# Four graph layers on one core: new adjacency landing times in the planner, and the last layer's weights folded later

## The chip, the cores and the metric

The kernel runs on one core of a Trainium2 chip. The metric is the time of one execution on the device in microseconds (us), lower is better. The engines are named as in the profile: PE is TensorE (PEld its weight loads), DVE is VectorE, ACT is ScalarE, POOL is GpSimd, and SP is the queue that issues most of the DMA transfers.

## The reference

32 graphs of 512 nodes with 128 features each share one 512x512 adjacency matrix `adj` of zeros and ones. Four layers follow one another, each behind a layernorm with ReLU and with a residual:

```python
# every layer: h = maximum(layernorm(x), 0);  x = x + layer(h)
# layer 0, attention: x_h = elu(h @ Wi + bi)
e = sigmoid(a_tgt[:, :, None] + a_src[:, None, :] + be) * (adj + 0.005 * (adj == 0))
agg = einsum('bij,bjh->bih', e, x_h);  self_part = x_h * sum(e, -1)
out = concat([elu(concat([agg, self_part]) @ Wn + bn), x_h]) @ Wm + bm
# layer 1, gated recurrence, 5 steps with in_matrix = out_matrix = adj
m = adj @ h;  av = concat([m, m]);  u3 = h @ u3_w.T
z = sigmoid(av @ w3_w.T + u3);  r = sigmoid(av @ w4_w.T + u3)
h = (1 - z) * h + z * tanh(av @ w5_w.T + (r * h) @ u5_w.T)
# layer 2: adj @ (h @ weight) + bias
# layer 3: weight_1 is 128 x 128 x 7; both adjacencies are adj, so
#   y = h @ w[:,:,0] + sum over k = 1..3 of adj^k h @ (w[:,:,k] + w[:,:,k+3])
```

In layer 3 the same powers of `adj` come twice, so that pairs of the seven weight slices can be added beforehand. These sums are the folded weights V[1] to V[3]; V[0] is the first slice alone.

## The kernel before

**Tiles.** The graphs are taken in eight groups of four. A tile of 512 columns holds one graph, either by token or by feature. The adjacency is loaded once in four chunks `A_nat` (L412), two on the SP queue and two on ACT's, and turned by 16 transposes (`adjacency_turned`, L601). DVE counts the entries that are neither zero nor one (`n_odd`, L592), PE adds the counts up (`count`, L621), and every engine reads the result and branches on it (L1184): with a binary adjacency the first arm runs. There `adj` goes through PE in the fp32r form, the other operand as a high and a low part (`parts`, L981), and the square of the adjacency is made at L974. Products with the small weights are full fp32 (`product`, L513).

**The order of the work.** Nothing is scheduled at run time. Every step is entered in a list with `op(engine, us, due, emit, reads, writes, ...)`: the engine, a cost in us, a due time and the tiles. `Plan.order` (L155) plays this list through with the costs and with landing times (`RESULT`, L76, or `result=` of a step), and each engine always takes the ready step with the earliest `turn`, which is its due time plus a `shift`. A step can't begin if its turn lies more than 110 us behind the oldest open one. What comes out is one fixed list of instructions for each engine; on the chip an engine works through its own list and waits at semaphores. A step whose input is late on the chip therefore holds up everything behind it on its engine.

Three things bend the order by hand. `A_LANDS` (L319) says when the four adjacency chunks are taken to land. `HEAD_NUDGES` (L25) is a list of seeds; for each, `nudge` (L255) adds random shifts of some us to steps that are due between 0 and 130, and `TAIL_NUDGES` does so behind 1430. And while the plan has no step for PE in its first 50 us (`FILL`), it puts in `plan.idle` (L375), a product of two tiles of ones into a spare bank, which nothing reads.

**Steps near the change.** Buffers are handed out by the plan: 38 `f` tiles of 128x512, eight PSUM banks `b`, five `x` groups, and so on. A layernorm is moments on DVE (L553 to L556), a power of -1/2 on POOL (L558), a small DVE operation (L562) and a scaling on ACT (L567). Between layouts by token and by feature a tile goes through DRAM: blocks are transposed on DVE (L462) and carried by two transfers (L464, then L475, L494 or L499). From the fifth graph on, a row of attention scores is spread over all partitions in the same way (`as_row`, L658). Sums over sources run as adding transfers on the POOL queue (`totals`, L672, and L802). The V tiles are made at L952: for each half of the outputs SP loads 448 columns of the raw weights into an `f` tile, and POOL makes four pieces from it, a copy (L960) and three additions (L962). They are read by `token_products` (L1093) in layer 3.

Of the kernel before, what the change touches and what calls it, by code (L numbers as in the profile page):

```python
# [21 lines left out]


HEAD, TAIL = 250.0, 1430.0
HEAD_NUDGES = (7100008, 7100429, 7300015, 7100544, 7100583, 7300139, 7300091, 7300684, 7300016, 7300033, 7300035,  # L25
    7300041, 7300077, 7300137, 7300140, 7300167, 7300172, 7300174, 7300178, 7300506, 7300199,
    7300249, 7300263, 7300279, 7300298, 7300305, 7300507, 14000074, 14000497, 7300344, 7300346,
    7300367, 7300389, 7300391, 7300393, 7300406, 7300423, 14000795, 7300482, 7300509, 7300510,
    7300530, 7300532, 7300539, 7300544, 14000157, 7300549, 7300551, 7300553, 7300562, 7300570,
    14000024, 14000577, 7300614, 7300629, 7300644, 14000027, 14000360, 7300654, 7300663, 7300681,  # L30
    14000347, 7300696, 14000026, 14000010, 14000014, 14000195, 14000023, 14000035, 14000039,
    14000042, 14000045, 14000046, 14000048, 14000088, 14000208, 14000563, 14000122, 14000125,
    14000164, 14000166, 14000167, 14000181, 14000182, 14000252, 14000186, 14000187, 14000189,
    14000198, 14000204, 14000210, 14000212, 14000213, 14000739, 14000219, 14000227, 14000231,
    14000243, 14000275, 14000289, 14000299, 14000304, 14000306, 14000385, 14000319, 14000324,
    14000325, 14000326, 14000333, 14000338, 14000345, 14000346, 14000355, 14000358, 14000364,
    14000665, 14000398, 14000472, 14000417, 14000426, 14000427, 14000432, 14000438, 14000440,
    14000451, 14000458, 14000463, 14000469, 14000485, 14000486, 14000515, 14000520, 14000521,
    14000647, 14000528, 14000531, 14000540, 14000596, 14000560, 14000561, 14000815, 14000569,
    14000570, 14000580, 14000589, 14000591, 14000597, 14000602, 14000605, 14000606, 14000609,  # L40
    14000629, 14000638, 14000654, 14000661, 14000689, 14000678, 14000681, 14000685, 14000686,
    14000697, 14000698, 14000700, 14000703, 14000708, 14000715, 14000716, 14000721, 14000723,
    14000725, 14000726, 14000732, 14000734, 14000744, 14000751, 14000753, 14000755, 14000788,
    14000796, 14000801, 14000804, 14000807, 14000808, 14000811, 14000816, 14000817, 14000818,
    14000822, 14000827, 14000829, 14000831, 14000836, 14000839, 14000842, 14000843, 14000847,
    14000849, 14000850, 14000851, 14000852, 14000853, 14000855, 14000856, 14000857, 14000860,
    14000864, 14000870, 14000871)
TAIL_NUDGES = ()


class Val:
# [18 lines left out]
class Plan:  # L70
# [21 lines left out]
    def op(self, eng, us, due, emit, reads=(), writes=(), two=None, keep=0, result=None,  # L92
           earliest=0.0, margin=0.0, hot=False):

        two = eng == "POOL" if two is None else two
        o = Op(eng, us, self.RESULT[eng] if result is None else result, emit, two, keep)
        o.earliest, o.margin, o.hot = earliest, margin, hot  # L100
        for v in reads:
            o.before.add(v.writer)
            if v.kind == "b" and v.readers and v.readers[-1].eng != eng:
                o.before.add(v.readers[-1])
        for v in writes:
            o.before.update(v.readers)
            if v.writer:
                o.before.add(v.writer)
            elif v.kind and v.slot is None:
                o.takes.append(v)  # L110
        for v in reads:
            v.readers.append(o)
        for v in writes:
            v.writer, v.readers = o, []
        o.vals = [v.whole or v for v in dict.fromkeys([*reads, *writes])]
        for v in o.vals:
            v.left += 1
        for v in [*reads, *writes, *o.vals]:
            self.vals[v] = True
        o.before -= {o, None}  # L120
        o.due = max([due, *(b.due for b in o.before)])
        if o.due > self.sure and o.result > 2.0:
            o.base, o.result = o.result, o.result + self.extra
        for b in o.before:
            b.after.append(o)
        self.ops.append(o)
# [147 lines left out]
def tile_four_graph_layers(  # L274
# [39 lines left out]
    FIRST_TREE, TREES, TREE = 4, 30, 52  # L314
    ONES, COPIES = 0, 32
    HALF = 2
    SQUARE, NAT = 11.0, 3.0
    BRANCHES = 0.75
    A_LANDS = (3.87, 3.05, 4.2, 4.0)  # L319

    T_MM, T_TR, T_NARROW, T_PASS = 0.86, 0.44, 0.224, 0.23
    T_VEC, T_COPY, T_ACT, T_DMA = 0.605, 0.5, 0.6, 0.45
# [2 lines left out]
    plan = Plan(slots, ahead=110.0, last=(B - 2) * PACE)  # L325
    op = plan.op
# [22 lines left out]
    def at(v):  # L349
        if v.tile is not None:  # L350
            return v.tile
        return places[v.kind][v.slot] if v.whole is None else at(v.whole)[:, v.part]
# [3 lines left out]
    def const(name, shape, dt=F32):  # L356
        if name not in const_tiles:
            const_tiles[name] = cpool.tile(shape, dt, tag=name, name=name)
        return Val(tile=const_tiles[name])
# [8 lines left out]
    ident, ones, neg_half = const("ident", [P, P]), const("ones", [P, P]), const("nhalf", [P, NC])  # L368
# [18 lines left out]
    def load(v, src, due, us=0.5, to=None, earliest=0.0, result=None, eng="SP"):  # L387
        queue = nc.sync if eng == "SP" else nc.scalar
        op(eng, us, due, lambda: queue.dma_start(at(v) if to is None else to(at(v)), src), [], [v],
           earliest=earliest, result=result)  # L390
        return v
# [20 lines left out]
    A_nat = [Val("f") for _ in range(NC)]  # L412
    for ic, v in enumerate(A_nat):
        load(v, adj.rearrange("(p c) n -> c p n", c=NC)[ic], -9.95, 0.45, earliest=0.3 * (ic % 2),
             result=A_LANDS[ic], eng=("SP", "ACT")[ic % 2])
    op("POOL", 0.2, -8.6, lambda: nc.gpsimd.tensor_copy(at(X[1])[:1, 0, :1], at(A_nat[1])[:1, :1]),
# [181 lines left out]
    def by_token(v):  # L598
        return at(v).rearrange("p (t c) -> p c t", c=NC)

    def adjacency_turned(due):  # L601
        banks = [Val("b") for _ in range(NC)]
        for pt in banks:
            pt.pieces = True
        for ic in range(NC):
            def turn(ic=ic):
                for jc, pt in enumerate(banks):
                    nc.tensor.transpose(at(pt)[:, ts(ic, P)], by_token(A_nat[ic])[:, jc, :], at(ident))
            op("PE", T_TR, due + ic, turn, [A_nat[ic], ident], banks)
        return banks  # L610

    adj_r = rows_of(const("adj_r", [P, NC, N], F32R).tile)
# [238 lines left out]
    def issue(operations):  # L851
        with tc.manual_schedule():
            for o in operations:
                o.emit()
# [6 lines left out]
    def arm(binary):  # L861
        with ExitStack() as stack:
# [11 lines left out]
            if not binary:  # L874
                issue(plan.order())
                return
            plan.nudge(0.0, 130.0, HEAD_NUDGES)
            order = [*plan.order(end=HEAD), *plan.order(end=TAIL)]
            plan.nudge(TAIL, 2000.0, TAIL_NUDGES)
            issue(order + plan.order())  # L880

    def list_rest(binary, pool):
# [70 lines left out]
        for half in range(2):  # L953
            t, outs = Val("f"), slice(half * P // 2, (half + 1) * P // 2)
            load(t, l3_w[:, outs, :].rearrange("i o k -> i (o k)"), 110, 1.3,
                 to=lambda t: t[:, : P // 2 * K])
            def fold(k, t, outs):
                w = at(t)[:, : P // 2 * K].rearrange("p (o k) -> p o k", k=K)
                if k == 0:
                    nc.gpsimd.tensor_copy(at(V[0])[:, outs], w[:, :, 0])  # L960
                else:
                    nc.gpsimd.tensor_tensor(  # L962
                        at(V[k])[:, outs], w[:, :, k], w[:, :, k + 3], op=ALU.add
                    )
            for k in range(4):
                op("POOL", 0.8, 110, lambda k=k, t=t, outs=outs: fold(k, t, outs), [t], [V[k]], earliest=60.0)


        if binary:
# [172 lines left out]
        def layer3(g, hT, uT, due, pace):  # L1142
            z = None
            stages = [[(hT, 2), (uT, 3)], [(hT, 0), (uT, 1)]] if binary else [[(hT, k)] for k in (3, 2, 1, 0)]
            for n, terms in enumerate(stages):
                new = []
                for ic in range(NC):
                    d = due + (n * NC + ic) * pace * 4 / len(stages)
                    very_last = g == NG - 1 and n + 1 == len(stages) and ic == NC - 1
                    for graphs in [range(HALF), range(HALF, G)] if very_last else [range(G)]:  # L1150
                        pz = started(terms, ic, d, z is None, graphs)
# [35 lines left out]
    with branch.Else():  # L1187
# [3 lines left out]
    nc.sync.dma_start(  # L1191
        out[B - G + HALF :].rearrange("b (p c) d -> c p b d", c=NC)[NC - 1],
        at(mask[0])[:, HALF * D :].rearrange("p (b d) -> p b d", d=D))

# [34 lines left out]
```

## Time and profile before

| | us |
|---|---|
| median of three runs | 1594.95 (1594.51 to 1596.13) |
| the profiled execution | 1594.3 |
| its span, first to last instruction | 1592.4 |
| PE busy | 1586.2 (100%) |
| DVE busy | 1414.9 (89%) |
| ACT busy | 1135.6 (71%) |
| POOL busy | 303.8 (19%) |

The clock that TensorE was granted is 0.999 of full speed over the span. In the busy times, matmuls that follow one another overlap at their ends, so a busy PE shows that it always had a matmul under way, not how much it got done. Starts of successive matmuls are the better measure. A matmul in fp32 is recorded as two matmuls, one in fp32r as one. In the head all engines work at once on several graphs, and the DMA queues carry 95 to 254 GB/s in the first 30 us.

### The profile page before, as it was taken

What the parts mean: (1) busy time and instruction counts of PE and PEld (TensorE: products, weight loads), DVE (VectorE), ACT (ScalarE), POOL (GpSimd) and SP (SyncE); (2) the same over time, 40 slices, a digit from 0 to 9 for tenths busy, and PEclk for the clock granted to TensorE, in tenths of its full rate; (3) what the DMA queues carried; (4) which work ended last, traced back from release to release, by engine and by line L of the source; (5) the groups of instructions that cost most, each with busy time, mean ns of one, the idle gap of its engine ahead of it and who ended that gap; (6) DMA issues with size and microseconds to landing.
All of it is one profiled execution on the core that took longest, in us unless ns stands there. A gap on an engine that the chain in (4) does not pass through costs nothing.

```text
span 1592.4 us, 21245 instructions
## 1 busy us (share of the span) xinstructions
PE 1586.2 (100%) x6279; PEld 1017.0 (64%) x6279; DVE 1414.9 (89%) x3367; ACT 1135.6 (71%) x2151; POOL 303.8 (19%) x297
## 2 busy tenths in 40 slices
PE   9999999999999999999999999999999999999998
PEld 7655555666666666666666666666666666656688
DVE  8999999999988999898999989989899898988772
ACT  7877776877776777677876777667687676755661
POOL 3322112212211212211222121221221111000010
PEclk9999999999999999999999999999999999999999
DMA  4465545564554556554555545555556554322221
GB/s 129 94 164 145 157 120 133 127 170 120 138 144 122 141 145 146 132 139 126 147 146 142 143 116 148 128 139 137 139 152 151 129 140 125 96 86 87 93 54 56
DMA packets 303062, 204.92 MB, mean 129 GB/s; under 512 B 94936, under 2 KB 245080, under 8 KB 302936
## 3 DMA queue, kind: packets, MB, share of 16 engines
q1 hardware_dynamic: 260808, 175.63, 36.0%
q0 software_dynamic: 39984, 26.38, 13.1%
q10 hardware_dynamic: 2144, 1.44, 0.3%
q8 instruction: 52, 0.85, 0.2%
q14 instruction: 74, 0.61, 0.1%
HBM read 96.41 MB, written 103.68 MB: 126 GB/s over the span
## 4 chain that ended last, share of the span: by engine, by line
PE 95%; DVE 2%; DMA 2%; ACT 0%; issue 0%; SPq 0%; DVEq 0%
PE b L521 43%; PE b L1018 26%; PE b L1093 7%; PE b L769 6%; PE b L1106 4%; PE b L830 3%; PE b L1081 2%; PE b L711 2%; PE b L821 2%; DMA f<-m 0%; DVE f L760 0%; DMA m<-f 0%; DMA f<-in_adj_dram 0%; DMA f<-d 0%; DVE f L648 0%; DVE f L646 0%
## 5 line engine op out<-in xcount | busy, mean ns | idle before, releaser
L510 ACT COPY f<-b 128x512 f32<-128x512 f32 x414 | 238.5, 585 | 179.2 <-PE b L1018 121.5
L558 POOL TENSOR_TENSOR s<-s,nhalf 128x4 f32<-128x4 f32 x128 | 156.0, 1221 | 768.8 <-DVE s L556 745.6
L1043 DVE TENSOR_TENSOR f<-f,b 128x512 f32<-128x512 f32 x320 | 213.5, 680 | 49.6 <-PE b L521 43.3
L1018 PE MATMUL b<-AQ,r 128*128 128x512 f32 x848 | 256.4, 432 | 0.0
L567 ACT ACTIVATE f<-x,s 128x128 f32<-128x128 f32 x496 | 204.2, 488 | 20.7 <-DVE s L562 18.4
L462 DVE STREAM_TRANSPOSE f<-f 128x512 f32<-128x512 f32 x246 | 206.5, 846 | 7.6 <-ACT f L567 6.3
L1018 PEld LDWEIGHTS b<-AQ,r 128*128 128x128 f32 x848 | 158.9, 188 | 69.5 <-issue 31.4
L1018 PE MATMUL b<-adj_r,r 128*128 128x512 f32 x640 | 193.7, 428 | 0.0
L526 ACT ACTIVATE f<-f,b4w 128x512 f32<-128x512 f32 x160 | 115.3, 721 | 96.4 <-DVE f L1043 95.6
L521 PE MATMUL b<-f,w4T 128*128 128x512 f32 x320 | 163.2, 593 | 0.1
L521 PE MATMUL b<-f,u5T 128*128 128x512 f32 x320 | 163.1, 593 | 0.0
L521 PE MATMUL b<-f,w5T 128*128 128x512 f32 x320 | 162.9, 592 | 0.0
L521 PE MATMUL b<-f,w3T 128*128 128x512 f32 x320 | 162.8, 592 | 0.0
L521 PE MATMUL b<-f,u3T 128*128 128x512 f32 x320 | 161.7, 592 | 0.0
L1018 PEld LDWEIGHTS b<-adj_r,r 128*128 128x128 f32 x640 | 120.0, 188 | 50.0 <-issue 21.3
L526 ACT ACTIVATE f<-b,b5w 128x512 f32<-128x512 f32 x160 | 109.5, 686 | 50.3 <-PE b L521 49.5
L526 ACT ACTIVATE f<-f,b3w 128x512 f32<-128x512 f32 x160 | 114.8, 719 | 35.7 <-DVE f L1043 35.0
L680 POOL DMA_DIRECT2D m<-f x78 | 71.0, 910 | 333.1 <-DVE f L1060 45.3
L1093 PEld LDWEIGHTS b<-V,f 128*128 128x128 f32 x1024 | 122.2, 192 | 16.0 <-issue 13.9
L1060 DVE TENSOR_TENSOR f<-f,f 128x512 f32<-128x512 f32 x160 | 109.2, 683 | 24.3 <-ACT f L526 23.6
L988 ACT CAST r<-f 128x512 fp32r<-128x512 f32 x197 | 120.5, 617 | 12.6 <-DMA f<-m 9.6
L992 DVE TENSOR_TENSOR r<-f,r 128x512 fp32r<-128x512 f32 x168 | 113.9, 682 | 12.9 <-ACT r L988 12.8
(138 smaller groups left out, 2665.9 us busy)
## 6 DMA issues: line engine op xcount, KB each, us to landing
m<-f SPq DMA_DIRECT2D x272, 256.0 KB
f<-m SPq DMA_DIRECT2D x186, 256.0 KB
m<-f POOLq DMA_DIRECT2D x78, 256.0 KB, 4.2
f<-m SPq DMA_DIRECT2D x240, 64.0 KB
f<-d SPq DMA_DIRECT2D x54, 256.0 KB
x<-in_x_dram SPq DMA_DIRECT2D x32, 256.0 KB
out_dram<-x SPq DMA_DIRECT2D x28, 256.0 KB
d<-y SPq DMA_DIRECT2D x54, 64.0 KB
```

The source lines that it names most:

```text
L462: op("DVE", us, due, lambda: nc.vector.transpose(view_out(at(blocks)), view_in(at(src))), [src], [blocks])
L510: op("ACT", us, due, lambda: nc.scalar.copy(at(t), at(src)), [src], [t])
L521: nc.tensor.matmul(to, at(w), of, start=start, stop=stop)
L526: op("ACT", us, due, lambda: nc.scalar.activation(at(dst), at(src), AF.Tanh, bias=at(bias), scale=scale), [src, bias], [dst])
L558: op("POOL", 1.2, due, lambda: nc.gpsimd.tensor_tensor(stat(SCALE), stat(VAR), at(neg_half), op=ALU.pow), [s, neg_half], [s], two=False)
L567: nc.scalar.activation(at(h)[:, ts(c, P)], at(X[b])[:, c, :], AF.Relu, bias=stat(SHIFT)[:, c : c + 1], scale=stat(SCALE)[:, c : c + 1],)
L988: op("ACT", T_COPY, due, lambda: nc.scalar.copy(part(hi), whole()), [src], [hi], keep=1)
L992: op("DVE", T_VEC, due, lambda: nc.vector.tensor_tensor(part(lo), whole(), part(hi).bitcast(F32), op=ALU.subtract), [src, hi], [lo], two=two)
L1018: nc.tensor.matmul(at(pa), at(part)[:, ts(jc, P)], view(at(columns[jc])), start=jc == n == 0, stop=jc == NC - 1 and n == PARTS - 1,)
L1043: op("DVE", T_VEC, d, lambda: nc.vector.tensor_tensor(at(s), at(u), at(pg), op=ALU.add), [u, pg], [s])
L1060: op("DVE", T_VEC, d, lambda c=c, h=h: nc.vector.tensor_tensor(at(c), at(c), at(h), op=ALU.subtract), [c, h], [c], two=True)
L1093: nc.tensor.matmul(at(pz)[:, ts(i, D)], at(t[i])[:, ts(ic, P)], at(V[k]), start=i == graphs[0] and n == 0, stop=last and i == graphs[-1] a ...
```

## The change

Four edits to the plan; no step is added or taken away, and no operation changes its form.

1. The landing times of the adjacency chunks are raised: 3.87, 3.05, 4.2, 4.0 become 4.2, 3.05, 4.7, 4.28.
2. The cost of one chunk's four transposes goes from 0.44 to 0.48.
3. The steps that fold the weights of the last layer, and the loads in front of them, get a shift of 155 and 145 us. Their due time stays 110, so that they compete for their engines as if they were due at 265 and 255.
4. The seeds of `HEAD_NUDGES` are replaced (208 by 469), and `TAIL_NUDGES` gets one.

```diff
@@
-HEAD_NUDGES = (7100008, 7100429, 7300015, 7100544, 7100583, 7300139, 7300091, 7300684, 7300016, 7300033, 7300035,
...
-TAIL_NUDGES = ()
+HEAD_NUDGES = (7100008, 91000240, 7100583, 7300139, 7300684, 7300016, 7300033, 7300041, 7300140, 7300172, 7300174,
...
+TAIL_NUDGES = (18500053,)
@@
+    FOLD = 155.0
...
-    A_LANDS = (3.87, 3.05, 4.2, 4.0)
+    A_LANDS = (4.2, 3.05, 4.7, 4.28)
@@
-            op("PE", T_TR, due + ic, turn, [A_nat[ic], ident], banks)
+            op("PE", 0.48, due + ic, turn, [A_nat[ic], ident], banks)
@@
             load(t, l3_w[:, outs, :].rearrange("i o k -> i (o k)"), 110, 1.3,
                  to=lambda t: t[:, : P // 2 * K])
+            plan.ops[-1].shift = FOLD - 10.0
...
             for k in range(4):
                 op("POOL", 0.8, 110, lambda k=k, t=t, outs=outs: fold(k, t, outs), [t], [V[k]], earliest=60.0)
+                plan.ops[-1].shift = FOLD
```

In the lists that result, the order on PE, DVE, ACT, POOL and SP differs almost everywhere behind the branch, since a nudged step moves all that follow it. The count of PE's rows goes from 6490 to 6491 over both arms. In the arm that runs, filler matmuls go from 35 to 36: the old list has 10 ahead of the first transpose and then 5, 3, 4, 2, 6, 1, 2, 1, 1; the new one has 11 and then 3, 3, 3, 1, 1, 7, 4, 1, 2. The loads of the raw weights go from places 32 and 35 of SP's list to 75 and 80, and the eight folding operations from places 37 to 48 of POOL's list to places 55 to 65.

## The prediction

> **What bounds the kernel now.** I read the page's busy times first, then the groups of matmuls, the chain of waits in order of time, busy time by stretch, and the timelines of the head. The page says that TensorE (PE) is hardly ever idle.
>
> ```profile
> PE 1586.2 (100%) x6279; PEld 1017.0 (64%) x6279; DVE 1414.9 (89%) x3367; ACT 1135.6 (71%) x2151; POOL 303.8 (19%) x297
> ```
>
> Busy PE isn't yet useful PE, because pipelined matmuls overlap. The chain gives the spacing of matmuls that follow one another (start, duration, what):
>
> ```profile
> 159.73 3.63 PE b L1018 x16
> 163.37 8.58 PE b L521 x20
> ...
> 1566.00 8.93 PE b L1093 x80
> ```
>
> 8.58/20 is 0.429 us for half of an fp32 product with 512 columns, 8.93/80 is 0.112 us for 128 columns; the x16 stretches of L1018 last 3.63 to 3.74, so 0.232 us for an fp32r matmul. From the groups of PE, kept apart by shape, there are 1992 of the first kind (L521, L769, L821), 2068 of the fp32r kind, some 2125 with 128 columns and 16 small ones. 1992 x 0.429 + 2068 x 0.232 + 2125 x 0.112 + 2 = 1574 us of useful work, which the change leaves alone. The span is 1592.4. The first transpose starts at 6.13 and the last matmul 4.5 before the end: 1574 + 6.1 + 4.5 = 1584.7. 7.7 us are left, and one group holds most of them:
>
> ```profile
> L375 PE MATMUL b<-ones 128*128 128x128 f32 x70 | 11.8, 320 | 1.0 <-DVE ones L370 1.0
> ```
>
> These are the filler matmuls of `plan.idle`, two records each. Twenty records run before the first transpose; the other 50 cost 50 x 0.112 = 5.6 us. So true waits are about 2.1 us. Starts of successive matmuls show where: 0.2 at 9.3, 0.3 at 19.6, 0.4 at 51.0, 0.2 at 73.0, 0.2 at 124.6, and crumbs. From 130 us to the end none.
>
> VectorE decides the head. In the chain, 29.6 to 51.3 us is an almost unbroken row of DVE work, of which two lines:
>
> ```profile
> 41.53 2.40 DVE f L760 x4
> 43.93 0.60 DVE x L541
> ```
>
> Busy time by stretch (length, then PE, PEld, DVE, ACT, POOL, clock, DMA share, GB/s) shows DVE full there and nearly full later:
>
> ```profile
> 20.00:30.00 10.00, 10.00 (x57) 7.46 (x58) 9.93 (x34) 8.99 (x21) 3.13 (x6) 1.00 0.33 95
> ...
> 130.00:160.00 30.00, 30.00 (x100) 16.74 (x99) 28.92 (x73) 23.57 (x46) 7.98 (x7) 1.00 0.57 143
> ```
>
> **A ceiling first.** The new PE order holds 36 fillers against 35: 11 before the first transpose (10 before) and 25 after it (25 before). Their 5.6 us stay. So even an order without one wait saves only the 2.1 us. 0.2% of 1594.95 is 3.2 us, about what a measurement of this kernel can tell from no change. Faster than that is out of reach unless the tail gets shorter. The tail keeps its cover: between the last layer 2 product and the last transpose both orders put 6.4 us of other matmuls, and both end on two half adds, DVE, one transfer.
>
> **The change part by part.**
>
> *Landings, and 0.48 for the adjacency transposes.* These are numbers of the planner; loads and first transposes stand as before. The eleventh filler adds two records at the 0.213 us spacing of that stretch: the last one would be done at 5.25 + 3 x 0.213 = 5.89. Cost nothing: PE waits for the adjacency, whose transfer in the chain ends at 6.00. Without that cover, 0.43.
>
> *Fillers ahead of the branch.* Timeline (start, duration, engine, line, operation):
>
> ```profile
> 8.29 1.28 PE L375 MATMUL b<-ones 128*128 128x128 f32 x10
> 8.34 0.08 DVE L594 DVE_READ_ACCUMULATOR f<-f 128x1 f32 x1
> ...
> 9.50 0.34 PE L623 MATMUL b<-ones,n_odd 128*1 128x1 f32 x8
> ...
> 9.87 0.14 DVE L628 CAST other<-b 1x1 int32<-1x1 f32 x1 [0.42 <-PE b L623]
> ```
>
> The count at L623 has its input at 8.42, but ten filler records stand ahead of it, and DVE then idles 0.42 for the count. The new order has three fillers there instead of five: 4 x 0.112 = 0.45 earlier, for DVE, for the branch and for all behind it. DVE's own work ends at 9.45, so 0.4 is gained.
>
> *The new order from there to 53 us.* I walked the new lists of PE, DVE, ACT and POOL by hand with spacings of this trace: two-input DVE work 0.61 (2.40/4 is 0.60), a layernorm's moments 1.3, its power on POOL 1.4 (1.03 to 1.51), an activation 0.60 to 0.63, the four scalings 1.66, a product 0.86, 0.15 to 0.25 from one engine to the next. Time minus useful work done is what PE has lost. At 18.1 us of useful work the old list had lost 12.0 (it is there at 30.09) and the new one 11.5. At 21.1: 12.45 and 12.4, because four fillers (0.9 us) stand before the second graph's aggregation, two stood there before. At 30.3: 12.8 and 12.4. At 39.5 to 40.1: 13.3 and 13.4, since three more fillers stand in that part and the first adjacency product of layer 1 has 8.9 us of PE work behind the add it depends on. The old list had 14 there. A hand walk is good to about 0.5, so **+0.1**, bounds -1.5 (all waits and crumbs up to here gone) and +2.5 (half a microsecond lost at five places where the walk saw PE and its input arrive within 0.2 of each other).
>
> *53 to 130 us.* PE lost 0.6 before, and the list behind it was dealt anew by the same planner. I take **0**, bounds -0.6 and +2 (five waits like the 0.4 at 51.0).
>
> *The fold leaves the head.* SP loses two loads at 18.55 and 20.86 us (1.24 and 0.61 to issue). Behind them come l2w, l2b, an X and the first transposed blocks up to 1.9 us sooner; no wait for l2w, l2b or that X stands in the waits, so nothing gained. On POOL eight operations go from between 58 and 76 us. They held DVE up there:
>
> ```profile
> 66.37 0.69 DVE L760 SCALAR_TENSOR_TENSOR f<-f,mask 128x512 f32<-128x512 f32 x1
> 66.97 1.10 DVE L562 SCALAR_TENSOR_TENSOR s<-s 128x4 f32<-128x4 f32 x1
> ```
>
> L562 has a median of 0.155: about 0.9 lost beside the folds at 67.07 to 68.3, 0.2 more in its neighbour. But DVE sat idle 2.4 us shortly before, and PE lost under 0.1 there: nothing gained.
>
> *The fold enters the steady part.* On SP the loads now stand at places 75 and 80, past 41 transfers, near 127 us by the old list. Right behind the first comes the spread of a graph's target row (L667 before), which is 1.24 late plus any wait for the load's f buffer. At 107 to 122 us the chain runs through just this kind of transfer (3.10, 3.68, 4.40 us) into ACT's tanh, and ends in PE's 0.2 us wait at 124.6. Bounds 0 and 1.2; I take 0.2, since most such spreads meet no waiting PE. On POOL the eight stand at places 55 to 65, around the accumulating transfers that the old list issues at 145.96, and two powers wait behind parts of them. The eight took 0.37 to 0.65, and one copy 3.29:
>
> ```profile
> 72.83 3.29 POOL L960 COPY V<-f 128x64 f32<-128x64 f32 x1
> ```
>
> All of them together 6.9 us. The largest block ahead of one power is six operations: 4 x 0.65 + 2 x 0.54 = 3.7 us, or 6.4 if the long copy is one of them. The planner has reserved 0.8 for each, 4.8 in all, so the power comes no later than planned, or 1.6 us later with the long copy. DVE may lose what it lost before, 1.1, up to 8 x 0.65 = 5.2 if each fold held it up; it idles 1.1 in those 30 us and PE's waits for DVE there are at most 0.5 at a time. I take **0.1**, near the 0.0 that PE lost at the old place; bounds 0 and 4. V is first read at 339 us, far behind either place.
>
> The Trainium skill ("SBUF — State Buffer", Who interferes with whom) says that a VectorE operation with two SBUF inputs and a GpSimd operation that reads SBUF exclude each other, and the second blocks fully. That speaks against moving the fold to where DVE is never idle. The trace agrees in part: L562 was blocked, but beside the 3.29 us copy five DVE operations kept their 0.60 us spacing, and the copy waited. By the rule alone DVE could lose 5.2 us and the sum would be up to 4 us higher.
>
> **Sum.** +0.1 + 0 + 0.2 + 0.1 = +0.4. The profiled execution took 1594.3 (span 1592.4 and 1.9 around), 0.65 below the median of the three runs, 1594.95. So 1594.7 for a profiled run, and **1595.3** as a median.
>
> **Rivals.**
> *Slower, the fold collides (12%).* A layernorm of the steady part waits behind the folds, or DVE loses most of the 5.2, in the stretch where DVE is 96% busy. For it: DVE has 1.1 us of idle in 30. Against: PE lost nothing beside the same eight operations before. It decides once DVE or a power is more than about 3 us late with PE waiting; then +3.5 to +5.7, 1598.5 to 1600.6.
> *Slower, a buffer or a transfer in the new head list (6%).* A product whose input goes through DRAM takes 7 us from DVE to landing (34.63 to about 41.6 in the trace; the walk leaves 1 us of slack). One that comes 3 us late with PE behind it: +3 to +4, about 1598.5.
> *Faster, the waits vanish (12%).* All 2.1 us of waits go: 1592.9. For it: 0.4 at the branch is sure. Against: DVE, not the fillers, limits 30 to 51 us, and its work is the same. Beyond 0.2% faster (3%) needs fillers that cost nothing or a shorter tail.
> *It doesn't do what it says.* The landings change only numbers; if PE meets the same waits one gets no change at all, 1594.95, inside the main case.
>
> **How the numbers follow.** The main case has 70%: 1594 to 1597, from the sum with two of the bounds met half way. With the faster rival it makes 79% for within 0.2% and 3% for faster; the two slower ones 18%. The range reaches to 1593.2, near the floor, and to 1598.8, into the slower cases.
>
> **What would show it.** Right: L375 with 72 records; L623 starting near 9.06 and the first L974 matmul near 10.45; PE time lost at 53 us equal within 1; the V operations of POOL at 130 to 165 us with no PE gap beside them; a PE busy time within 2 us of 1586. Wrong: a gap over 1 us between matmuls anywhere after 60 us, a power on POOL that starts over 3 us after its DVE line, or a tail over 4.5 us.

## The result, and the profile after

The changed kernel took 1598.12 us in the median of 22 runs (1594.98 to 1599.52), the kernel before 1594.93 in as many beside it (1593.16 to 1596.13). The ratio is 1.0018, 95% interval 1.0012 to 1.0024. By the ratio that is 2.9 us more (1.9 to 3.8): inside the range of the prediction and within the 0.2% that it called no change, but clearly above the forecast of 1595.3. So the question is which terms of its sum were too small.

The profiled execution of the changed kernel took 1596.77 with a span of 1593.9. Line numbers are about 30 higher than before (L375 is L405, L521 is L551, L623 is L653, L974 is L1006). The page's busy times:

```profile
PE 1586.9 (100%) x6281; PEld 1017.2 (64%) x6281; DVE 1415.4 (89%) x3367; ACT 1136.7 (71%) x2151; POOL 302.9 (19%) x297
```

PE is as busy as before, within 0.7 us. What changed shows in the groups of PE kept apart by shape (busy time, mean ns, idle time before them and what ended it):

```profile
L551 PE MATMUL b<-f,w3T 128*128 128x512 f32 x320 | 163.0, 593 | 1.4 <-ACT f L540 1.4
L551 PE MATMUL b<-f,u5T 128*128 128x512 f32 x320 | 162.7, 592 | 0.5 <-DVE f L1082 0.5
...
L405 PE MATMUL b<-ones 128*128 128x128 f32 x72 | 12.2, 323 | 1.0 <-DVE ones L400 1.0
```

The filler group has the 72 records that were expected. The idle times in the first two rows are new waits, at three places: two for a copy by ACT and one for DVE's L1082. The waits of PE from 60 to 170 us say the same (waiting line, what it waited for, us, times, longest); for the kernel before this view is empty.

```profile
PE b L551 <- ACT f L540: 1.4, 2, 0.9
PE b L551 <- DVE f L1082: 0.5, 1, 0.5
```

The head up to the branch went as predicted. The timeline:

```profile
8.55 0.08 DVE L624 DVE_READ_ACCUMULATOR f<-f 128x1 f32 x1
...
9.11 0.34 PE L653 MATMUL b<-ones,n_odd 128*1 128x1 f32 x8
...
9.58 0.14 DVE L658 CAST other<-b 1x1 int32<-1x1 f32 x1
...
10.51 0.61 PE L1006 MATMUL b<-adj_r,q 128*128 128x512 f32 x1
```

The count starts at 9.11 instead of 9.50 and the square of the adjacency at 10.51 (forecast 9.06 and 10.45).

To place the losses I take time minus useful work again, from the starts of successive matmuls, fillers counted as lost. At 60 us this kernel had lost 11.96, the kernel before 12.32. Then 0.74 goes at 69.5 us, 1.04 at 91.5 and 0.66 at 155.7, where the kernel before lost next to nothing. From 160 us on the two run side by side, up to a tail that is 0.4 shorter in the changed kernel (last matmul 4.13 before the end, 4.50 before the change). The chain of waits in order of time (start, duration, what) shows what stands behind the second of these:

```profile
78.99 5.27 DMA d<-y
...
84.33 3.68 DMA f<-d
...
88.04 0.73 ACT f L787
...
88.78 2.97 DMA f<-m
...
91.78 0.62 ACT r L1020
92.40 0.50 ACT f L540
...
92.94 0.70 PE b L551
```

`DMA d<-y` is the first half of a row of scores that goes through DRAM (`as_row`), `f<-d` the half that spreads it. The first half took 4.84 us at 59.11 and 5.27 at 78.99; the same two hops took 2.68 and 2.52 in this trace of the kernel before. ACT, which works its list in order, waits for the spread row. Once ACT is through with it SP issues `f<-m`, ACT waits for that too, and PE for ACT's copy. The third wait comes from VectorE:

```profile
154.89 0.70 DVE L492 STREAM_TRANSPOSE f<-f 128x512 f32<-128x512 f32 x1
155.52 1.22 DVE L1082 SCALAR_TENSOR_TENSOR f<-f,f 128x512 f32<-128x512 f32 x1
```

L1082 takes 0.65 elsewhere. The folds run on POOL at just that time:

```profile
154.83 1.11 POOL L993 TENSOR_TENSOR V<-f 128x64 f32<-128x64 f32 x1
155.16 1.01 POOL L991 COPY V<-f 128x64 f32<-128x64 f32 x1
155.41 2.34 POOL L993 TENSOR_TENSOR V<-f 128x64 f32<-128x64 f32 x2
```

One more thing stands in no busy time. Time minus span is 1.8 us in the kernel before (median of 88 runs, 1.74 to 1.92) and 2.9 in the changed one (22 runs, 2.82 to 3.13): 1.1 of the 2.9 us lie outside the span. The DMA view behind the last instruction (1593.9 to 1597) holds one packet in the changed kernel, and none in the kernel before:

```profile
DMA packets 1, 0.01 MB, mean 3 GB/s; under 512 B 0, under 2 KB 0, under 8 KB 0
## 3 DMA queue, kind: packets, MB, share of 16 engines
q14 instruction: 1, 0.01, 1.0%
```

It is a fetch of 8 KB of code, 2.08 us after the last instruction.

So I had three candidates: late hops in the new head list (H), folds beside the steady part (F), and the place of the code (C).

### The profile page after: what moved, and what is told of

The parts are those of the page before. It is cut to its first block, busy times and chain, and to the rows that moved or that the text cites. A ratio compares the mean times of both kernels' runs of the same rounds, so it can differ in the third digit from the quotient of the medians.

```text
span 1593.9 us, 21224 instructions
## 1 busy us (share of the span) xinstructions
PE 1586.9 (100%) x6281; PEld 1017.2 (64%) x6281; DVE 1415.4 (89%) x3367; ACT 1136.7 (71%) x2151; POOL 302.9 (19%) x297
## 4 chain that ended last, share of the span: by engine, by line
PE 91%; DVE 4%; DMA 2%; ACT 1%; issue 0%; POOL 0%; SPq 0%; DVEq 0%
PE b L551 42%; PE b L1050 25%; PE b L1125 7%; PE b L799 6%; PE b L1138 4%; PE b L860 3%; PE b L1113 2%; PE b L851 1%; PE b L741 1%; DVE f L790 1%; DMA d<-y 1%; DMA f<-d 0%; DVE f L492 0%; DMA f<-m 0%; DMA m<-f 0%
## 5 line engine op out<-in xcount | busy, mean ns | idle before, releaser
L1050 PE MATMUL b<-AQ,r 128*128 128x512 f32 x808 | 249.6, 431 | 0.0
L1050 PEld LDWEIGHTS b<-AQ,r 128*128 128x128 f32 x808 | 151.5, 188 | 67.6 <-issue 31.8
L1050 PE MATMUL b<-adj_r,r 128*128 128x512 f32 x584 | 182.3, 429 | 0.0
L551 PE MATMUL b<-f,w3T 128*128 128x512 f32 x320 | 163.0, 593 | 1.4 <-ACT f L540 1.4
L551 PE MATMUL b<-f,u5T 128*128 128x512 f32 x320 | 162.7, 592 | 0.5 <-DVE f L1082 0.5
L551 PE MATMUL b<-f,w4T 128*128 128x512 f32 x320 | 163.0, 592 | 0.0
L551 PE MATMUL b<-f,w5T 128*128 128x512 f32 x320 | 162.6, 592 | 0.0
L551 PE MATMUL b<-f,u3T 128*128 128x512 f32 x320 | 161.9, 592 | 0.0
L1050 PEld LDWEIGHTS b<-adj_r,r 128*128 128x128 f32 x584 | 109.4, 188 | 46.6 <-issue 18.4
L1125 PE MATMUL b<-V,f 128*128 128x128 f32 x1024 | 123.9, 275 | 0.0
L1020 ACT CAST r<-f 128x512 fp32r<-128x512 f32 x190 | 116.5, 616 | 9.8 <-DMA f<-m 7.7
```

The lines of the kernel that those rows point to most:

```text
L551: nc.tensor.matmul(to, at(w), of, start=start, stop=stop)
L1020: op("ACT", T_COPY, due, lambda: nc.scalar.copy(part(hi), whole()), [src], [hi], keep=1)
L1050: nc.tensor.matmul(at(pa), at(part)[:, ts(jc, P)], view(at(columns[jc])), start=jc == n == 0, stop=jc == NC - 1 and n == PARTS - 1,)
L1125: nc.tensor.matmul(at(pz)[:, ts(i, D)], at(t[i])[:, ts(ic, P)], at(V[k]), start=i == graphs[0] and n == 0, stop=last and i == graphs[-1] a ...
```

## The experiments

**1. The changed kernel again.** No edit.

> The changed kernel once more, unaltered, for a second trace of it. All theories: 1597.6 to 1598.6 us against about 1594.9 for the kernel before. Theory H (late hops): PE's list again stands 0.5 us or more near 69 us and near 91 us, both times behind the row that goes through DRAM, whose first transfer takes 4.5 us or more from its issue to the issue of the second. Theory F (folds): PE stands 0.5 us or more near 155 us, beside the folds. Rival theory S (scatter): the three waits of the first trace sit elsewhere in this one or are under 0.3 us each, and only the sum repeats.

1598.37 us (1596.35 to 1600.35, 11 runs), ratio 1.0019 (1.0010 to 1.0028). The same three waits stand in the second trace: 0.71 at 69.7, 1.56 at 91.6, 0.66 at 157.5. The hops took 4.79 and 5.22. There is also a fourth, at 125.6:

```profile
PE b L551 <- ACT f L540: 1.9, 2, 1.4
PE b L1050 <- DVE r L1024: 0.8, 1, 0.8
PE b L551 <- DVE f L1082: 0.5, 1, 0.5
```

The wait for the folds is the same in both; the others are of the same kind but not of the same size. So the rival S falls for these two traces, though experiment 6 has one in which the first two of the three waits are missing. The sizes vary with the landings of one execution.

**2. Folds of one column.**

```diff
-                    nc.gpsimd.tensor_copy(at(V[0])[:, outs], w[:, :, 0])
+                    nc.gpsimd.tensor_copy(at(V[0])[:, at_one], w[:, :1, 0])
```

(an excerpt; the additions likewise, and V is filled with a constant at the start)

> The changed kernel with each of the eight folds cut to one column; the last layer's folded weights are a constant written at the start instead, so the fold itself is left out. The lists of all engines stand as in the changed kernel. Theory F (the folds beside the steady part are the main cost): 1595.0 to 1595.6 us, as before the change. Theory H (late hops in the new head list are the main cost, the folds cost the 0.66 us of the wait at 155.6 us): 1597.2 to 1597.7 us. Theory S: 1598 us, no difference.

1596.39 us (1594.51 to 1597.20), 1.0008 (0.9999 to 1.0017). That is 1.7 less than the changed kernel, between the two expectations. In its trace the wait at 155 is gone, and L1082's counterpart has its normal length:

```profile
155.14 0.66 DVE L1088 SCALAR_TENSOR_TENSOR f<-f,f 128x512 f32<-128x512 f32 x1
```

The waits near 70 and 91 stayed (0.68 and 0.93). Time minus span stayed at 3.0.

**3. Hops ahead of their neighbours.** In SP's list, the one or two 256 KB transfers just ahead of a hop's first half go behind it:

```diff
 DMACopy d_128<-y_123 4x32x128
+DMACopy m_136<-f_86 128x512
...
-DMACopy m_136<-f_86 128x512
```

> The changed kernel with two places of SP's list turned round: the 64 KB transfer that starts each of the first two rows through DRAM (issued at 59.1 and 79.0 us) goes ahead of the one or two 256 KB transfers that stood directly before it. Theory H: the hop is down from 4.9 and 5.3 us to 2.6 to 3.2 us, the waits at 69 and 91 us (0.74 and 1.04 us) go to under 0.3 us, and the time is 1596.2 to 1596.8 us. Theory F: 1598 us, unchanged. Theory A (not SP's transfers but GpSimd's adding transfers beside the hop slow it): the hop stays above 4 us and the time at 1597.6 to 1598.6.

1597.91 us, 1.0022 (1.0013 to 1.0031): no gain. The first halves came down only to 3.60 and 3.75. And the transfer put behind the first hop then took 4.24; SP stood waiting for it ahead of the hop's second half, which was issued at 64.8 instead of 64.0. The wait near 70 us stayed at 0.71, and near 89 us PE lost 1.11, behind a transfer `f<-m` that was issued at 83.28 and took 4.94. Here the transfer that went second was late in its turn. So it isn't the order on SP's queue alone.

**4. The folds moved in the kernel before.** All lists as before, only the two loads and the eight folds plucked out and put where the plan reaches 146 and 155 us (an excerpt; the raw weights go into an `x` tile here).

```diff
+        for o in [o for o in order if o.late]:
+            order.remove(o)
+            n = next(n for n, x in enumerate(order) if getattr(x, "start", 0) >= o.late and not x.late)
+            order.insert(n, o)
```

> The kernel before with its own lists, in which only the two loads of the last layer's weights and the eight folds are taken out of the head and put where the steady part has reached 146 and 155 us by the planner's times. Theory H: the move alone costs what the folds cost beside the steady part, 0.3 to 0.8 us: 1595.2 to 1595.7 us. Theory F: 2 to 3 us: 1597 to 1598. A gain of more than 0.3 us would show that the folds cost something in the head, which I put at nothing.

1595.70 us (1594.09 to 1597.00), 1.0004 (0.9995 to 1.0013). Between 141 and 160 us PE lost under 0.1. In the old list the folds meet no VectorE operation that PE waits for. But this trace, with PE's, DVE's and ACT's lists exactly those of the kernel before, shows two waits that the profiled execution of the kernel before lacks:

```profile
PE b L521 <- ACT f L510: 0.8, 1, 0.8
PE b L830 <- DVE f L648: 0.7, 1, 0.7
```

Both lie between 121 and 126 us, behind the folds' old place and before their new one. The second row is the earlier of the two, and experiments 5 and 12 show it too (0.85 lost at 121.7 and 122.0), where the folds are not moved. So the old list has waits for landings as well, and the profiled execution that I read was a lucky one: of the 88 runs of the kernel before that were timed beside the experiments, 12 had a span as short.

**5, 6 and 9. The place of the code.** The arm for a weighted adjacency is never run on this input, but its code stands between the arm that runs and the end. I put idle copies into it, on one engine at a time.

```diff
             if not binary:
                 issue(plan.order())
+                for _ in range(10):
+                    nc.vector.tensor_copy(at(ones)[:1, :1], at(ones)[:1, :1])
                 return
```

> The kernel before with ten copies of one element added on VectorE in the arm for a weighted adjacency, which this input never runs: nothing executed changes, only the place of what stands behind that arm in VectorE's code, by the ten instructions by which the changed kernel's VectorE program is longer. Theory C (code placement on VectorE makes the 1.1 us that the changed kernel spends outside the span): time minus span goes from 1.8 to 2.9 us and a code fetch of 8 KB shows about 2 us behind the span's end; the time is 1.1 us above the kernel before at an unchanged span. Rival: the place of another engine's code, or the lists themselves, make it: time minus span stays at 1.8 us.

> The changed kernel with eight such copies on ScalarE in the arm that is never run, which puts the end of ScalarE's code where it stood in the kernel before (its program is eight instructions shorter after the change). Theory C with VectorE: time minus span stays at 2.9 us. Theory C with ScalarE: it goes to 1.8 us.

> The changed kernel with 118 copies of one element on VectorE in the arm that is never run, which puts the end of VectorE's code at the place within an 8 KB block (128 instructions of 64 bytes) that it has in the kernel before. Theory C: time minus span falls from 2.9 to 1.8 us, the code fetch behind the span's end is gone, the time is 1596.8 to 1597.3 us. Rival (ten instructions more were enough to make it in the kernel before, but in this one something else makes it): 2.9 us still, 1598.

| kernel | VectorE's program, instructions beyond the last full 128 | time minus span, us | code fetch behind the span |
|---|---|---|---|
| before | 60 | 1.80 | none |
| 5: before, VectorE + 10 | 70 | 2.72 (2.49 to 2.96) | at +1.68 |
| changed | 70 | 2.91 (2.82 to 3.13) | at +2.08 |
| 6: changed, ScalarE + 8 | 70 | 2.89 (a single run) | at +2.32 |
| 9: changed, VectorE + 118 | 60 | 1.82 (1.75 to 1.84) | none |

The program of VectorE is 7356 instructions in the kernel before and 7366 in the changed one, as built, at 64 bytes each in the built file, so that a fetch of 8 KB holds 128. Ten instructions that are never executed, put into the kernel before, gave the fetch behind its end and 0.9 us more outside the span (median 1596.12 against 1595.0; 1.0007, 0.9998 to 1.0017, at an unchanged span of 1593.3 in the mean). 118 more in the changed kernel took both away: 1596.63 us, 1.0009 (1.0000 to 1.0018), with waits of PE at the same places. In the DMA view behind the last instruction of number 5 the same single packet stands:

```profile
DMA packets 1, 0.01 MB, mean 2 GB/s; under 512 B 0, under 2 KB 0, under 8 KB 0
## 3 DMA queue, kind: packets, MB, share of 16 engines
q14 instruction: 1, 0.01, 0.6%
```

C holds, on VectorE. In the kernels of the other experiments the 1.8 and the 2.9 go with the fetch too, without exception: at places 54 to 61 and 75 there is none, at 70 there is. The trace of number 6 will matter again: its lists are those of the changed kernel, and yet PE's waits from 60 to 170 us were this one alone:

```profile
PE b L551 <- DVE f L1084: 0.5, 1, 0.5
```

**7. Each fold twice.**

```diff
-                        nc.gpsimd.tensor_copy(at(V[0])[:, outs], w[:, :, 0])
+                    for _ in range(2):
+                        nc.gpsimd.tensor_copy(at(V[0])[:, outs], w[:, :, 0])
```

(the additions likewise)

> The changed kernel with each of the eight folds done twice, one behind the other (the second writes the same values). Theory F (the folds cost about 1.7 us in the span, as leaving them out saved): 1599.3 to 1600.5 us. Theory H (they cost the 0.66 us wait of the trace and little else, and GpSimd has room behind them): 1598.4 to 1599.2 us, with a second PE wait of 0.3 to 1 us between 157 and 165 us. Rival: nothing, since the matmuls near 157 us wait for one VectorE instruction alone: 1598.1.

1596.86 us (1594.99 to 1597.78), 1.0009 (1.0000 to 1.0018): no theory's number. Twice the work cost less than once. In its trace L1082's counterpart came at 157.21 with 0.65 us, and it was two L1026 operations, which nobody on PE was waiting for, that took 1.58 together. The wait of 0.66 is not there:

```profile
PE b L551 <- ACT f L540: 1.7, 2, 1.1
PE b L1052 <- DVE r L1026: 0.6, 1, 0.6
```

So the folds have no price for each fold. In these traces it is one hit on one operation, when the two meet. Where that hit is missing, here and in experiment 2, the span is 1593.6 and 1593.2 in the mean, against 1594.8 for the changed kernel: 1.2 and 1.65 less, more than the 0.7 that the hit costs PE in the traces.

**8. No fillers behind the branch.**

```diff
-            issue(order + plan.order())
+            issue([o for o in order + plan.order() if o is not plan.idle])
```

> The kernel before without the 17 filler matmuls (34 records of 0.112 us, 3.8 us) that its list holds behind the branch. If they stand where PE would wait anyway, as the prediction put it when it took the ceiling of a gain from them: 1594.8 to 1595.3 us and true waits of 3.8 us more in the head. If they delay the work behind them: down to 1591.3 us. If the clock falls in the waits: 1596 us or more, and granted clocks under 1.0 before 53 us.

1595.20 us (1593.86 to 1597.88), 1.0004 (0.9995 to 1.0013). At 60 us PE had lost 11.9 with 34 filler records fewer, 11.7 to 12.3 with them. Behind 53 us the list is that of the kernel before, and in this trace PE lost 4.7 more by 142 us: the second hop took 4.81 here. The fillers stand in time in which PE waits anyway, and the granted clock from 10 to 53 us was 1.00 without them.

**10. Lighter adding transfers beside the hops.**

```diff
-                        at(sums[0]), at(e), accum_op=ALU.add)
+                        at(sums[0])[:8], at(e)[:8], accum_op=ALU.add)
```

(and the same for the first graph whose sums go through `totals`; the row sums of the two graphs are left incomplete)

> The changed kernel with the adding transfers of GpSimd's queue cut from 128 to 8 partitions for graphs 3 and 4 (those at 58 to 85 us), so that the row sums of these two graphs miss most of their terms; all lists stand as they were. Theory A (these transfers beside the hop make it late): the hop is down from 4.8 and 5.3 us to 3.7 us or less, the waits near 70 and 91 us are gone, and the time is 1596.2 to 1597 us. Rival (the 256 KB transfers on SP's own queue make it late, or the second half of the hop does, which takes 3.9 us): the waits stay, 1597.6 to 1598.4 us.

1594.94 us (1593.53 to 1596.10), 0.9998 (0.9989 to 1.0007). Between 60 and 120 us PE lost nothing. What is left of PE's waits from 60 to 170:

```profile
PE b L551 <- DVE f L1082: 0.5, 1, 0.5
PE b L551 <- DMA f<-m: 0.3, 1, 0.3
```

This kernel's VectorE program happens to end at place 75, so 1.1 of the 3.2 us saved belong to C. In the span, its mean is 1593.05 against 1594.84 for the changed kernel. Theory A holds for the hops: with the adding transfers whole, six traces of the changed kernel's lists (result, experiments 1, 2, 6, 7 and 9) have them at 4.48 to 5.39, and here they took 3.01 and 3.56. That fits what the Trainium skill ("DMA: Bandwidth & Descriptors", Queues, rings and completion order) says, that each DMA engine takes packets from its queues in turn: a small transfer shares the engines with whatever other queues hold.

Two things keep this from being the price of the change. In experiment 6, with the adding transfers whole and hops of 4.48 and 4.56, PE lost 0.6 between 60 and 140 us, as little as in the profiled execution of the kernel before; so a hop of 4.5 us need not make PE wait, and one trace without waits does not show that the cut removed them. And the same cut was not tried in the kernel before, which loses time in that stretch too. The 1.8 us of the span are what these adding transfers cost the changed kernel, not what the change added.

**11. The same hop lengthened in the kernel before.** An excerpt; `write` is the step of the first half, and `spread` becomes the step of the second:

```diff
+        def spread():
+            if write.start < 100.0:
+                write.emit()
+            nc.sync.dma_start(at(t), at(row)[:, None, :].to_broadcast([COPIES, P // COPIES, N]))
```

> The kernel before, in which the first two rows through DRAM are written twice, the second time just ahead of the transfer that spreads them: the hop of 2.7 us becomes about 5 us, as it is after the change; nothing else is altered. Theory H: PE waits of 0.5 to 1 us show near 66 to 72 us and 85 to 93 us, and the time is 1595.6 to 1596.8 us. Rival (the list of the kernel before has room for a hop of 5 us, and only the new order makes it decide): within 0.3 us of the kernel before.

1600.02 us (1599.83 to 1600.75, 6 runs), 1.0031 (1.0019 to 1.0043), more than expected. With its second writing, the row stood in DRAM 6.7 and 5.4 us after the first issue. PE then lost 0.86 and 0.49 at 68 to 70 us, 1.40 and 0.43 at 89 to 94, and again at 125 to 129. The chain:

```profile
64.52 2.93 DMA f<-d
...
67.47 0.72 ACT f L760
...
70.42 0.70 PE b L521
```

So the old list has no room for two late hops either. What it had was mostly short ones: the first took 2.7 to 2.8 in all six of its traces, the second 2.4 to 2.5 in four. In experiments 8 and 12 the second took 4.81 and 4.25 with the old list. There an adding transfer of GpSimd had been issued 0.6 and 0.4 us ahead of the hop, and one of SP's own 0.7 and 0.6 ahead; in the profiled execution the adding one came 0.4 behind it. PE lost 1.09 near 88 us in the first of the two and nothing there in the second.

**12. The landings alone.** The first two edits of the change, with the old seeds.

> The kernel before with the new landing times and the new duration of the four transposes alone, without the new seeds and without moving the folds. In the arm that runs, the lists then differ from those of the kernel before in filler matmuls alone: eleven instead of ten ahead of the first transpose, three instead of five ahead of the count. As the prediction has it, this part costs nothing: 1594.8 to 1595.3 us, the count of odd entries about 0.45 us earlier. Rival: the filler more ahead of the first transpose stands in the way, or the earlier branch gains: a difference of 0.3 us or more either way.

1595.55 us (1594.06 to 1597.03), 1.0003 (0.9994 to 1.0013). The count began at 8.8, the square at 10.2. This part costs nothing that can be measured and gains nothing.

## Why the prediction was right, and where its sum was not

**The range held**, and no change beyond 0.2% came out as forecast, because the bounds of two steps were wide: 53 to 130 us (up to +2) and the folds beside DVE (up to +4). The middle was 2.8 us too low, and 1.1 of that stands in no term, so that the range held is in part luck. Two of the signs that were named went against it: there are gaps over 1 us between matmuls after 60 us (by the starts 1.04 was lost at 91.5, and 1.56 and 2.07 there in experiments 1 and 9), and PE has a gap beside the folds. The other signs came as named: 72 filler records, the count at 9.11, the square at 10.51, the time lost at 53 us, the busy time of PE. What the runs put against the terms:

| step | predicted | measured |
|---|---|---|
| landings, eleventh filler | 0 | 0 (experiment 12) |
| new order up to 53 us | +0.1 | 0: lost at 60 us 11.96 to 12.49 in traces of the new list, 11.67 to 12.32 of the old |
| 53 to 130 us | 0 | +0.4 or nothing, see below |
| fold leaves the head | 0 | no gain seen (experiment 4) |
| spread behind the load on SP | +0.2 | 0 |
| folds beside DVE | +0.1 | +0.7 |
| tail | 0 | -0.4, see below |
| outside the span | not in the sum | +1.1 |

*Outside the span.* The step that failed was "span 1592.4 and 1.9 around", taken over as a constant. It is the largest single term and has nothing to do with the order of the work: with the new lists VectorE's program came out ten instructions longer.

*Folds beside DVE.* The mechanism was named, with the right rows and the right place; the value was taken "near the 0.0 that PE lost at the old place". The term was mis-sized. At the new place one operation on PE's path met them: 1.22 instead of 0.65, and PE lost 0.70 to 0.74 between 140 and 160 us in the traces of the result and of experiments 1, 6 and 9. DVE as a whole did not lose the 5.2 that the rule of the Trainium skill ("SBUF — State Buffer", Who interferes with whom) would allow. By the rule the one that comes second is fully blocked. The measured excess of 0.57 us on this one agrees in kind, and experiment 7 shows that the bill depends on which operation is hit.

*53 to 130 us.* "PE lost 0.6 before" was read from one execution. Between 60 and 140 us, four traces of the old list (the profiled one, experiments 4, 5 and 12) lost 0.6, 2.5, 2.1 and 2.9. Four of the new one (the profiled one, 1, 6 and 9) lost 1.8, 3.4, 0.6 and 3.7. The means are 2.0 and 2.4. Experiment 8, whose list is the old one behind 53 us, lost 4.7, and experiments 2 and 7, whose lists are the new ones up to 140 us, 2.0 and 3.0; with these the means are 2.6 and 2.4. So the traces scatter by far more than they differ, and no cost of the new order shows there. What failed is the reading of one execution as the list's own loss. The rival "a transfer in the new head list" had a mechanism that is there: two hops 2.2 and 2.8 us longer than in the profiled execution before. But it stayed far below its price of 3 to 4, for PE lost 0.7 and 1.0 behind them, and the old list has waits of the same kind at 121 to 126 and 139 us.

*Spread behind the load.* The load of the raw weights stands right behind a hop's first half, as said. It was issued at 129.74 for 0.48 us while that hop was under way until 131.61, and the spread went out at 131.63. The wait of SP covered it, and so there is no 1.24.

*Tail.* The prediction let it stand as it was. With the old lists the last matmul starts 4.5 to 4.9 us before the end (six traces), with the new ones 4.1 to 4.5 (eight). From the point at which 150 us of useful work are done, near 165 us, to the end the four new traces named above take 1427.9 in the mean and the four old ones 1428.3. No run changes the tail's seed alone, so what made it shorter is not shown.

*Ceiling and fillers.* Experiment 8 confirms that the fillers cost next to nothing in themselves, 0.4 at 60 us at most, so the 3.8 us of the 34 records stand almost wholly in time in which PE would have waited. The faster rival, in which waits vanish, did not come.

*A reading.* Seven of the eight folds of the kernel before took 0.37 to 0.67 us and one copy 3.29; added up that is 7.5 and not 6.9. The sum does not use it.

**The sum.** 1.1 + 0.7 + 0.4 - 0.4 is 1.8, and less if nothing is put for 53 to 130 us. In the span, 45 runs of the changed lists (result, experiments 1, 6 and 9) have a mean of 1594.84, 88 of the kernel before 1593.31: 1.5, and with the 1.1 outside 2.6, against 2.9 by the ratio. So the traces account for 0.7 of the 1.5 at most. A part of the rest is the choice of traces: the spans of the four new ones are 1.0 above those of the four old ones in the mean, and not 1.5. Cutting the folds took 1.65 from the span and cutting the adding transfers 1.8, each about the whole excess and each good to about 0.7; they can't both own it, and the second was not tried in the kernel before. How much belongs to the folds and how much to the landings in the new head list stays open beyond the waits that the traces show. The new seeds were never run without the later folds.

None of these kernels beats the kernel before. The changed one with VectorE's code moved (experiment 9) is the fastest of the new lists that do all the work, among those timed more than once: 1.0009 of the kernel before against 1.0018, some 1.4 us (experiment 7 has the same ratio).

## What to carry to other kernels

Before judging a change of a few tenths of a per cent, subtract the span from the time in both kernels: here the difference came from where VectorE's program ends and not from the order of the work, and idle instructions in a part that isn't run showed it and took it away. Read more than one trace of the kernel before: one profiled execution shows one draw of the landings, and a list that seems to wait nowhere can lose 2 us in the next. A small hop through DRAM on the path deserves a look at what else is under way at that time: here cutting another queue's traffic shortened it about as much as putting its own queue's transfers behind it. And before a saving is called the price of a change, the same cut should be made in the kernel before.

## What the runs showed of the hardware that was not expected

- A fetch of 8 KB of code after the last instruction, 1.7 to 2.3 us behind it, with 0.9 to 1.1 us more time outside the span. It came with VectorE's program ending at place 70 of a 128-instruction stretch and not at 54 to 61 or 75. On the page of the profile the fetches of this queue are 74 of 0.61 MB together, 8 KB each; the other queue that fetches code has 52 of 0.85 MB, 16 KB each. The Trainium skill ("Runtime: NRT & Kernel Launch", Instruction fetch mechanics) has blocks of 16 KiB and calls the cost of crossing one mostly hidden; the fetches of this queue are half of that here, and at the end of the program the cost showed.
- A 64 KB transfer into DRAM took 2.5 to 2.7 us in the kernel before, where the last transfer ahead of it had been issued 2.3 us or more earlier. It took 4.8 and 5.3 in the changed one, where an adding transfer of GpSimd's queue and one or two of SP's own, of 256 KB each, had been issued within 1 us ahead, and 4.3 and 4.8 with the old list where both stood within 0.7 us ahead (experiments 12 and 8). With the adding ones cut to 16 KB it took 3.0 and 3.6; with SP's own put behind it, 3.6 and 3.75.
- Twice the folding work on GpSimd cost nothing above once (1.0009 of the kernel before, against 1.0018). In that trace the VectorE operation that PE waits for took 0.65 us and not 1.22.
